# Two groups of score matmuls put side by side, with two of their tiles in another part of PSUM

## The chip, the cores and the metric

The kernel runs on one core of one Trainium2 chip. The metric is the device time of one execution in microseconds (us). Before the change it is 2308.98 us, the median of three runs (2308.58 to 2309.19).

## The reference

Two attention layers follow each other on a tensor `x` of 8 images, 32 x 32 positions (N = 1024 rows) and 256 channels, all in float32.

- Layer 0 has four heads of 256 channels each: `softmax(q k^T / 16) v` per image and head, then a product with `W_out` and the addition of `x`.
- Layer 1 has one head. Its keys `f` and queries `g` have only 32 channels, its values `h` 256: `s = g f^T`, `b = softmax(s)`, `y = gamma * (b h) + x`.

```
f, g, h = x Wf + bf, x Wg + bg, x Wh + bh
s = einsum('bik,bjk->bij', g, f)
o = einsum('bij,bjd->bid', softmax(s, axis=-1), h)
y = gamma * o + x
```

So a matmul of layer 1's scores contracts over 32 channels, a quarter of the 128 rows of TensorE's array. The product of the probabilities with the values contracts over 1024 positions.

## The kernel before, in words

**Steps.** The work is a list of steps, each a unit and a block of 512 query rows. An image has four layer-0 units (one for each head) with two blocks each; from the second image on, a layer-1 unit of the image before stands among them, with two blocks too. Its place is given by `behind`: after the second head, and for the last image at the end of the list. Layer 1 of the last image (image 7) is run by code of its own after the loop. Thus seven layer-1 units, of images 0 to 6, go through the loop, and that of image 6 is the last unit of the list: in its second block the next step, `nxt`, is None.

**Order within a step.** In every step, pieces of several stages are put on a scale with `put(tasks, *at)`: a piece with a lower number is issued earlier (line 1073 sorts them). The engines PE (TensorE), DVE (VectorE) and ACT (ScalarE) get their instructions in exactly this order, each engine its own share of it. An engine takes them one after another; what one engine waits for from another is settled by semaphores.

**Layer 1's second block (`blk == 1`).** This step holds, in its order: the accumulation of the layer-0 output of the step before last (`L700`, on DVE, at 0.5), the first group of scores (0.5), four sums for the small output product (`L691`, on DVE, 0.6 to 0.9), the first product of block 0 (1), the second group of scores (2), the next head's queries (from 2.5), the small output product (from 3), and block 0's further products (4, 6, 8).

- A group of scores is `task` inside `Layer1.scores` (line 810 on): four matmuls (L820), each with 32 of the 128 array rows and its own PSUM tile of 512 columns, then four exponentials (L829) on ACT that read these tiles. Two groups make a block's 1024 keys.
- A product is `row_products.task` (L908): eight float32 matmuls into one PSUM tile; DVE then takes the reciprocal of the row's sum (L916) and scales and adds the tile to `x` (L918). After L918 the PSUM tile is free.
- The other matmuls, of layer 0, come from `seven` (L255), with sums on DVE (L272) and copies on ACT (L278, L284). Names: `psx_q, psy_q, psz_q` are the next head's queries, `psx_o, psy_o` the small output product, `psx_y, psy_y, psz_y` layer 0's product with the values.
- GpSimd (POOL) adds up row sums over the partitions (L626) and issues the accumulating DMA (L703) after L700.

**PSUM.** Tiles are given out by two pools of one bank a tile: `ps` with six tiles and `psm` with two. `psm` holds the small products: `psx_o` and `psy_o` (with `psz_o` in the same tile), and the projections. A pool hands out its tiles in turn; the first instruction that writes a tile waits until the last reader of the tile's former content has ended.

```
y=2, yt=1, invb=1, e=2, u=2, w=1, eh=1, uh=1, eo=1, uo=1, st=2, r=8, line=4, ps=6, psm=2,
```

On TensorE every float32 matmul is recorded as two passes, each a weight load (PEld) and a matmul (PE), so eight matmuls show as x16 and the four of a score group as x8.

Of the kernel before, what the change touches and what calls it, by code (L numbers as in the profile page):

```python
# [16 lines left out]
P = 128  # L17
# [3 lines left out]
def kernel(  # L21
# [59 lines left out]
    NB = 512  # L81
# [29 lines left out]
    def tile_of(tag, shape, name):  # L111
        return pools[tag].tile(shape, F32, tag=tag, name=name)
# [340 lines left out]
    def residual(b):  # L453


        def piece(c):
            if c == 0:
                x1T_of[b] = tile_of("xT", [P, CC, N], f"x1T_{b}")
            nc.scalar.activation(
                x1T_of[b][:, c, :], xT_of[b][:, c, :], AF.Identity, bias=boutT_sb[:, c : c + 1]  # L460
            )

        return [partial(piece, c) for c in range(CC)]
# [48 lines left out]
    class Layer0:  # L512
# [46 lines left out]
        def scores(self, blk):  # L559

            half = NT // 2
            exp = partial(nc.scalar.activation, func=AF.Exp, scale=SCALE)
            tasks = []

            def p():
                if blk not in self.p:
                    self.p[blk] = tile_of("s", [P, NT, NB], f"p_{self.name}_{blk}")
                return self.p[blk]

            for g in range(0, half, 2):  # L570
                def out(j, e, g=g):
                    return p()[:, j * half + g : j * half + g + 2, ts(e, HB)]

                def after(g=g, out=out):
                    both = p()[:, half + g : half + g + 2, :]
                    exp(both, both)  # L576
                    exp(out(0, 1), out(0, 1))

                tasks += seven(
                    f"{self.name}_{blk}_{g}", NB, 2,  # L580
                    lambda number, g=g: [
                        (i, xblocks[self.b][number][:, ts(g + i, P)],
                         self.qblocks[blk][number])
                        for i in range(2)
                    ],
                    {
                        "11": partial(out, 0, 0), "12": partial(out, 0, 1),
                        "21": partial(out, 1, 0), "22": partial(out, 1, 1),
                    },
                    WIDE, exp, after,  # L590
                )
            return tasks
# [125 lines left out]
    class Layer1:  # L718
# [87 lines left out]
                ), last,  # L806
            )

        def scores(self, blk):

            n = f"{self.name}_{blk}"
            four = P // CK
            soft = Softmax(self, blk)
            exp = partial(nc.scalar.activation, func=AF.Exp, scale=self.scale)

            def task(j0):
                pms = []
                for r in range(four):
                    pm = tile_of("ps", [P, NB], f"ps_{n}_{j0 + r}")
                    nc.tensor.matmul(  # L820
                        pm,
                        lhsT=self.f[ts(r, CK), ts(j0 + r, P)],
                        rhs=self.g[ts(r, CK), ts(blk, NB)],
                        start=True,
                        stop=True,
                    )
                    pms.append(pm)
                for r, pm in enumerate(pms):
                    (exp if blk < self.direct else nc.scalar.copy)(soft.tile()[:, j0 + r, :], pm)  # L829

            tasks = [partial(task, j0) for j0 in range(0, NT, four)]
            if blk < self.direct:
                return tasks, []
            have = [
                partial(soft.have, [(j0, j0 + 2), (j0 + 2, j0 + four)])
                for j0 in range(0, NT, four)
            ]
            return tasks, have + soft.pieces()
# [115 lines left out]
    pm = tile_of("psm", [P, NB], "pm_idle")  # L954
# [27 lines left out]
    def is_l0(s):  # L982
        return s is not None and isinstance(s[0], Layer0)

    def step(k):
        return steps[k] if 0 <= k < len(steps) else None
# [4 lines left out]
    for i, (a, blk) in enumerate(steps):  # L991
        l0 = isinstance(a, Layer0)
        one, two, nxt = step(i - 1), step(i - 2), step(i + 1)
        places = []

        def put(tasks, *at):
            assert len(tasks) == len(at)
            places.extend(zip(at, range(len(places), len(places) + len(at)), tasks))

        if l0:  # L1000
            put(a.scores(blk), 0, 2, 4, 6, 8, 10)
        else:
            tasks, _ = a.scores(blk)
            put(tasks, *((0.5, 2.4) if blk == 0 else (0.5, 2)))
        if is_l0(two):
            u, k = two
            put(u.products_of[k][2:], 1 if l0 else 0)
            if nxt is None:
                put([partial(u.invert_all, k)], 2.2)
            put([partial(u.invert, k)], 3.4 if l0 else 2.7)  # L1010
            ysums, tasks, adds[i] = u.project(k)
            put(ysums, *((1.1, 1.2, 1.3, 3.3) if l0 else (1.1, 1.2, 1.3, 2.5) if blk == 0 else
                         (0.6, 0.7, 0.8, 0.9)))
            put(tasks, *((3, 5.5, 7) if l0 else (4.5, 6, 7.2) if blk == 0 else
                         (3, 5, 7) if nxt else (1.9, 3.1, 4.1)))
            if nxt is None:
                put(adds[i], 4.2)
        if i - 1 in adds:
            put(adds[i - 1], 0.5 if l0 or blk == 1 else 2.3)
        if is_l0(one):  # L1020
            u, k = one
            sums, keys = u.sums(k)
            u.products_of[k] = u.products(k)
            put(sums, *((2.1, 3.2, 4.2, 5.6) if l0 else (0.8, 2.2, 3.5, 6.1)))
            put(keys, *((6.3, 6.6, 7.6, 8.7) if l0 else (6.3, 7.6, 8.3, 8.7)))
            put(u.products_of[k][:2], *((5, 9) if l0 else (4, 5)))
        elif one is not None:
            put(one[0].products(one[1]), *((3, 5, 7, 9) if l0 else (1, 4, 6, 8) if nxt else (1, 3, 4, 8.5)))
        if i == 0:
            put(fold[0][2:] + fold[1], -2, -1, 0.5, 1.5, 2.5, 4.5, 6.5, 8.5)  # L1030
            put(first_sums[:2], 8.4, 9.4)
        if i == 1:
            put(first_sums[2:], 1.4, 3.4)
            put(fold[2], 0.5, 2.6, 3.5, 5.5, 7.5)
            put([partial(nc.vector.tensor_scalar, bh_sb, bh_sb, gamma_sb, None, ALU.mult)], 8.5)

        if l0 and blk == 0:
            put(a.query_sums(1), 3.5, 4.3, 4.4, 5.3)
        if is_l0(nxt) and blk == NBLK - 1:
            put(nxt[0].queries(), *((2.5, 4.5, 6.5) if not l0 else  # L1040
                                    (1.5, 2.5, 4.5) if is_l0(two) else (0.5, 2.5, 5.5)))
            put(nxt[0].query_sums(0), *((6.7, 6.9, 7.3, 7.6) if not l0 else
                                        (5.4, 6.4, 7.2, 7.4) if is_l0(two) else (6.4, 7.2, 7.3, 7.4)))

        if l0 and a.h == 0 and blk == 1:
            put(residual(a.b), 5.3, 7.3)
        if l0 and a.h == 0 and blk == 1 and a.b > 0:
            put(value_sums(a.b), 1.4, 2.4, 3.4, 4.4)
        if l0 and a.h == 1 and blk == 0 and a.b + 1 < B:
            load_x(a.b + 1)  # L1050
        if is_l0(nxt) and nxt[0].h == 2 and nxt[1] == 0 and nxt[0].b + 1 < B:
            moves, turned = turn_rows(nxt[0].b + 1)
            put(moves[:4], 1, 2.5, 4, 5.5)
        if l0 and a.h == 2 and a.b + 1 < B:
            if blk == 0:
                put(moves[4:], 0.5, 1.5, 2.5, 3.5)
                put(turned, 6.4, 7.4, 8.4, 9.4)
            else:
                put(key_sums(a.b + 1), 0.5, 0.6, 6.4, 7.4)

        if l0 and a.b > 0 and a.h == behind(a.b) - 1:
            if blk == 0:
                moves, turned1 = turn_back(a.b - 1)
                put(moves[:4], 3, 4.5, 6, 7.5)
            else:
                put(moves[4:], 4, 5.5, 7, 8.5)
                tasks, moves = nxt[0].queries_apart()
                put(tasks, 1.5)
                put(moves, 1.6, 1.7, 1.8, 1.9)
        if not l0 and blk == 0:  # L1070
            put(a.values("ps"), 0.9, 1, 2.3, 3, 6.5)
            put(turned1, 2.5, 2.9, 4.2, 5.1)
        for _, _, t in sorted(places, key=lambda x: x[:2]):
            t()
# [94 lines left out]
    with tc.If(bad > 0), ExitStack() as general:  # L1169
# [7 lines left out]
        for b in range(B):  # L1177
# [3 lines left out]
            for h in range(HEADS):  # L1181
                a = General0(b, h, bout_sb)
# [4 lines left out]
            a = Layer1(b)  # L1187
# [37 lines left out]
```

## Time and profile before

| what | value |
|---|---|
| median of 3 runs | 2308.98 us |
| profiled execution, its own time | 2309.19 us |
| its span, first to last instruction | 2307.3 us |
| PE busy | 2298.1 us (100%) |
| DVE busy | 1653.9 us (72%) |
| ACT busy | 579.7 us (25%) |
| POOL busy | 319.9 us (14%) |
| L820, the scores of layer 1 on PE | x256, 36.6 us busy |
| L908, the products of layer 1 on PE | x1024, 232.1 us busy |
| mean granted TensorE clock | 0.999 |

The span is what the profiler saw between the first and the last instruction; the execution's own time has 1.9 us more around it. The timeline gives, for each engine, the start in us from the span's start, the length, the line, the tiles (written, then read) and how many instructions were merged into the row; a bracket at the end is the idle time before it and what ended it. A matmul's recorded length is longer than its turn on the array, since matmuls overlap: what counts is the distance between the starts.

### The profile page before, as it was taken

The numbers are of one execution on the slowest core, as the hardware profiler recorded it, in microseconds if no ns is written. First come the engines' busy times: TensorE is split into PE (matmuls) and PEld (weight loads), VectorE is DVE, ScalarE is ACT, GpSimd is POOL, SyncE is SP. The second block draws the span as 40 slices with busy tenths as digits, with TensorE's granted clock in tenths as the row PEclk, the third lists the DMA queues.
The fourth block names the chain that finished last, engine by engine and source line by source line (L and its number), as shares of the span: only waits on it lengthen the run. The fifth ranks groups of instructions, "written<-read, shape, count | busy, mean of one in ns | idle before, by whom it ended". The sixth has DMA issues, their size and how long they took to land.

```text
span 2307.3 us, 27302 instructions
## 1 busy us (share of the span) xinstructions
PE 2298.1 (100%) x10256; PEld 1892.6 (82%) x10256; DVE 1653.9 (72%) x2951; ACT 579.7 (25%) x1009; POOL 319.9 (14%) x206
## 2 busy tenths in 40 slices
PE   9999999999999999999999999999999999999999
PEld 7888888788878888778887888878888788888877
DVE  6787787577775777657776677766777667777763
ACT  2222222222221222212232122221222222222222
POOL 0111112011120111101121011210112101111211
PEclk9999999999999999999999999999999999999999
DMA  4211123301233013220132201322113210131222
GB/s 137 33 28 25 23 39 51 74 15 28 34 51 70 15 28 47 47 62 15 28 55 43 58 15 28 58 42 55 19 24 58 42 37 19 28 46 24 40 44 62
DMA packets 240380, 94.82 MB, mean 41 GB/s; under 512 B 204464, under 2 KB 209456, under 8 KB 240240
## 3 DMA queue, kind: packets, MB, share of 16 engines
q1 hardware_dynamic: 220784, 55.23, 12.1%
q0 software_dynamic: 19456, 37.76, 9.3%
q8 instruction: 83, 1.36, 0.4%
q14 instruction: 57, 0.47, 0.1%
HBM read 29.76 MB, written 8.65 MB: 17 GB/s over the span
## 4 chain that ended last, share of the span: by engine, by line
PE 99%; DMA 1%; SPq 0%; DVE 0%; issue 0%; ACT 0%
PE psy_y L255 14%; PE psy L255 14%; PE pa_l L908 10%; PE psx L255 10%; PE psx_y L255 10%; PE psz_y L255 10%; PE psz L255 10%; PE psy_o L255 6%; PE psy_q L255 4%; PE pr_v_l L494 3%; PE psx_o L255 2%; PE psx_q L255 2%; PE psz_q L255 2%; PE ps_l L820 1%; PE pm_fg L770 1%; DMA w<-in_L_conv_W_out_dram 0%
## 5 line engine op out<-in xcount | busy, mean ns | idle before, releaser
L626 POOL PARTITION_ALL_REDUCE rb<-rs x64 | 206.6, 3228 | 1436.2 <-DVE rs L624 906.1
L255 PE MATMUL psx<-q,x0T 128*128 128x256 f32 x1024 | 263.6, 380 | 0.0
L255 PE MATMUL psy<-qs,xs 128*128 128x256 f32 x1024 | 262.9, 379 | 0.0
L255 PE MATMUL psz<-q,xs 128*128 128x256 f32 x1024 | 262.8, 379 | 0.0
L576 ACT ACTIVATE p<-p 128x1024 f32<-128x1024 f32 x128 | 135.3, 1057 | 494.6 <-DVE p L272 494.6
L255 PE MATMUL psy_y<-p,xt 128*128 128x256 f32 x1024 | 241.9, 379 | 0.0
L255 PE MATMUL psx_y<-p,x 128*128 128x256 f32 x1024 | 241.9, 379 | 0.0
L908 PE MATMUL pa_l<-v_l,s_l 128*128 128x257 f32 x1024 | 232.1, 381 | 0.0
L255 PEld LDWEIGHTS psx<-q,x0T 128*128 128x128 f32 x1024 | 193.9, 190 | 45.2 <-issue 20.7
L255 PEld LDWEIGHTS psx_y<-p,x 128*128 128x128 f32 x1024 | 194.7, 190 | 34.0 <-issue 8.6
L908 PEld LDWEIGHTS pa_l<-v_l,s_l 128*128 128x128 f32 x1024 | 193.9, 190 | 34.2 <-issue 6.8
L255 PEld LDWEIGHTS psy<-qs,xs 128*128 128x128 f32 x1024 | 194.6, 190 | 26.7 <-DVE q L272 0.4
L255 PEld LDWEIGHTS psy_y<-p,xt 128*128 128x128 f32 x1024 | 194.7, 190 | 26.3
L255 PEld LDWEIGHTS psz<-q,xs 128*128 128x128 f32 x1024 | 194.7, 190 | 26.3
L284 ACT ACTIVATE p<-psx 128x512 f32<-128x512 f32 x128 | 76.4, 597 | 363.8 <-PE psx L255 363.6
L272 DVE TENSOR_TENSOR u<-psy,e 128x512 f32<-128x512 f32 x128 | 88.1, 688 | 86.9 <-ACT e L278 75.5
L703 POOL DMA_DIRECT2D x1T<-o x64 | 78.1, 1220 | 427.2 <-DVE o L700 304.5
L255 PE MATMUL psy<-qs,x0T 128*128 128x256 f32 x512 | 132.3, 381 | 0.3 <-DVE v L272 0.3
L272 DVE TENSOR_TENSOR v<-psy,e 128x512 f32<-128x512 f32 x128 | 88.3, 690 | 53.0 <-PE psy L255 51.6
L255 PE MATMUL psy_y<-ss,xt 128*128 128x256 f32 x512 | 121.4, 380 | 0.1
L255 PE MATMUL psz_y<-ss,x 128*128 128x256 f32 x512 | 121.0, 379 | 0.0
L255 PE MATMUL psz_y<-ss,xt 128*128 128x256 f32 x512 | 121.0, 379 | 0.0
(139 smaller groups left out, 3404.6 us busy)
## 6 DMA issues: line engine op xcount, KB each, us to landing
x1T<-o POOLq DMA_DIRECT2D x64, 512.0 KB, 5.0
invb<-inv SPq DMA_DIRECT2D x63, 256.0 KB
x<-x1T SPq DMA_DIRECT2D x256, 32.0 KB
out_dram<-x SPq DMA_DIRECT2D x15, 512.0 KB
x<-in_x_dram SPq DMA_DIRECT2D x14, 512.0 KB
x0T<-x SPq DMA_DIRECT2D x224, 32.0 KB
fg<-v_l POOLq DMA_DIRECT2D x56, 64.0 KB, 2.1
w<-in_L_conv_W_qkv_dram SPq DMA_DIRECT2D x4, 512.0 KB
```

The costliest lines, as they stand in the source:

```text
L255: nc.tensor.matmul(banks[k][:, ts(i, w)], lhsT=lhsT, rhs=rhs, start=first and n == 0, stop=True, skip_group_check=True,)
L272: nc.vector.tensor_tensor(dst, shaped(banks[k]), shaped(other), ALU.add)
L284: copy(outs["11"](), shaped(banks["x"]))
L494: nc.tensor.matmul(pm[:, ts(j, C)], lhsT=src()[:, c, ts(2 * t2 + j, P)], rhs=w()[:, c, :], start=(c == 0), stop=(c == CC - 1),)
L576: exp(both, both)
L626: nc.gpsimd.partition_all_reduce(t, r.rearrange("p e i -> p (e i)"), P, bass_isa.ReduceOp.add)
L703: nc.gpsimd.dma_start(x1T_of[self.b][:, :, ts(blk, NB)], o, accum_op=ALU.add)
L770: nc.tensor.matmul(pm[ts(k, half)], lhsT=w[:, c, :], rhs=x1T_of[b][:, c, ts(k, NB)], start=(c == 0), stop=(c == CC - 1),)
L820: nc.tensor.matmul(pm, lhsT=self.f[ts(r, CK), ts(j0 + r, P)], rhs=self.g[ts(r, CK), ts(blk, NB)], start=True, stop=True,)
L908: nc.tensor.matmul(pm[:, : C + 1], lhsT=p[:, j, ts(ti, P)], rhs=v[:, j, : C + 1], start=(j == 0), stop=(j == NT - 1),)
```

## The change

Two things change for the second block of a layer-1 unit, where a next step exists:

- both groups of scores are put behind the first product, one right after the other (at 2 and 2.05 in place of 0.5 and 2);
- the first two tiles of the block's scores come from the `psm` pool in place of `ps`.

The condition holds for the units of images 0 to 5. In image 6's unit `nxt` is None, and the closing code for image 7 calls `scores` without the new argument; both stay as they were. What is computed does not change, nor the number of instructions that do it. Three lines more stand in the file, so L820 becomes L822, L829 becomes L831, L908 becomes L910, L916 and L918 become L918 and L920.

```diff
-        def scores(self, blk):
+        def scores(self, blk, small=0):
...
                 for r in range(four):
-                    pm = tile_of("ps", [P, NB], f"ps_{n}_{j0 + r}")
+                    tag = "psm" if j0 + r < small else "ps"
+                    pm = tile_of(tag, [P, NB], f"ps_{n}_{j0 + r}")
                     nc.tensor.matmul(
...
         else:
-            tasks, _ = a.scores(blk)
-            put(tasks, *((0.5, 2.4) if blk == 0 else (0.5, 2)))
+            pair = blk == 1 and nxt is not None
+            tasks, _ = a.scores(blk, 2 if pair else 0)
+            put(tasks, *((0.5, 2.4) if blk == 0 else (2, 2.05) if pair else (0.5, 2)))
```

## The prediction

> **What bounds the kernel now.** I read the page's head first, then the waits, then the timeline of each engine around one of the changed places (times below are us from the start of the span).
>
> ```profile
> span 2307.3 us, 27302 instructions
> PE 2298.1 (100%) x10256; PEld 1892.6 (82%) x10256; DVE 1653.9 (72%) x2951; ACT 579.7 (25%) x1009; POOL 319.9 (14%) x206
> ```
>
> TensorE is busy for 2298.1 of 2307.3 us, and in the list of waits no wait of PE's matmuls passes 1.1 us in its total. So there is no slack on PE: whatever PE gains or loses at one place is gained or lost at the end. The work is the same in every image: layer 1's second block begins at 400.97, 684.91, 968.84, 1252.95, 1536.89 and 1820.82, 283.9 us apart each time. The second of these, on PE:
>
> ```profile
> 684.38 0.59 PE L255 MATMUL psz_y<-ss,x 128*128 128x256 f32 x2
> 684.91 1.14 PE L820 MATMUL ps_l<-fg 32*128 32x512 f32 x8
> 685.98 3.73 PE L908 MATMUL pa_l<-v_l,s_l 128*128 128x257 f32 x16
> 689.64 1.14 PE L820 MATMUL ps_l<-fg 32*128 32x512 f32 x8
> 690.71 1.13 PE L255 MATMUL psx_q<-x0T,wqk 128*128 128x512 f32 x2
> ```
>
> See the starts: first group of scores (four float32 matmuls, two passes each), product, second group, psx_q. In VectorE's timeline of the same stretch see when it reaches the product's reader, the last line:
>
> ```profile
> 685.96 2.90 DVE L700 TENSOR_TENSOR o<-o,invb 128x1024 f32<-128x1024 f32 x1
> 688.77 0.41 DVE L691 TENSOR_TENSOR yt<-y 128x256 f32<-128x256 f32 x1
> 689.22 0.42 DVE L691 TENSOR_TENSOR y<-y 128x256 f32<-128x256 f32 x1
> 689.68 0.42 DVE L691 TENSOR_TENSOR yt<-y 128x256 f32<-128x256 f32 x1
> 690.13 0.42 DVE L691 TENSOR_TENSOR yt<-y,yt 128x256 f32<-128x256 f32 x1
> 690.48 0.16 DVE L916 RECIPROCAL inverse<-pa_l 128x1 f32<-128x1 f32 x1
> 690.67 0.48 DVE L918 SCALAR_TENSOR_TENSOR x<-pa_l,inverse,x 128x256 f32<-128x256 f32 x1
> ```
>
> GpSimd's, ScalarE's and the weight loads' timelines have the rest: the reduction that L700 runs beside, the exponentials, and the load of psy_q, the matmul that today takes over the product's bank:
>
> ```profile
> 685.54 3.23 POOL L626 PARTITION_ALL_REDUCE rb<-rs  x1 [15.99 <-issue]
> 686.11 2.06 ACT L829 ACTIVATE s_l<-ps_l 128x512 f32<-128x512 f32 x4 [7.25 <-PE ps_l L820]
> 690.80 2.06 ACT L829 ACTIVATE s_l<-ps_l 128x512 f32<-128x512 f32 x4 [2.62 <-PE ps_l L820]
> 691.27 0.19 PEld L255 LDWEIGHTS psy_q<-xs,wt 128*128 128x128 f32 x1 [0.27 <-issue]
> ```
>
> [...] In mid-stream a 512-column matmul of two passes takes 0.86 us (698.15 to 699.01) and a product 3.46 us (694.69 to 698.15); here the product takes 3.66 us (685.98 to 689.64), 0.11 more for a weight load that nothing hides [...]. [...] L700 takes 1.22 us as a rule (median 1216 ns) and 2.90 us here, ending just after the reduction does (685.54 + 3.23 = 688.77).
>
> **What is removed.** A group in four row tiles costs, beyond its two passes: 0.09 drain + 1.07 (684.91 to 685.98) + 0.11 load of the next full-array matmul - 0.86 = 0.41 us. With both groups side by side one way in and one way out fall away. What a seam between two groups of one mode costs, no row shows: at least 0 (the second pass's loads inside a group are hidden already), at most the 0.11 of an open load. I take 0; it is hidden in the wait below in any case. If nothing waited, the gain is 0.41 us a place (0.30 at the other end), and places there are six: images 0 to 5. Image 6's second block is the last step (nxt is None) and image 7 goes through the closing code; both keep the old form. 6 x 0.41 = 2.5 us.
>
> **What is added: a wait for the product's bank.** PSUM's ps pool has six tiles and hands them round in turn. After the change pa_l takes one, then come ps_l 2 and 3 of the first group and ps_l 4 to 7 of the second, since only 0 and 1 go to psm: with pa_l as number one, ps_l 7 is number seven and gets pa_l's bank. (The built program agrees: exactly this matmul has a wait on VectorE and TensorE that was psy_q's before; there psy_q was seventh.) That bank is free when L918 has read it. VectorE's order of work is the same instruction by instruction, and nothing ahead of L918 in it waits for a PE instruction later than psz_y, so L918 ends when it does now, at 690.67 + 0.48 = 691.16 to the nearest reading. It is late because VectorE first finishes L700, held up by GpSimd, and four L691, not because of the product.
>
> PE in the new order:
> - psz_y's stream ends at 684.82 (eight of 0.216 from 683.09). The product follows with no change of mode and ends its stream at 684.82 + 3.46 = 688.28.
> - Drain 0.09, first group's load at 688.37, streaming 688.48 to 689.34.
> - The second group's tiles 4 to 6 can start; ps_l 7 cannot. Its load begins at 691.16 + 0.11 = 691.27 (0.11 is what lay between L918's end and psy_q's load in the trace of before).
> - From the first load of a group to the next full-array load is 1.07: psx_q's load at 692.34.
>
> Before, that load was at 690.71. Each place loses 692.34 - 690.71 = 1.63 us: a wait of 2.04 (689.23, when the load would have begun without a wait, to 691.27) less the 0.41. The bounds: the release by semaphore could take 0.05 or 0.2 instead of 0.11, and the seam or a split of the passes 0.1: 1.5 to 1.8.
>
> Behind the held matmul stands everything on PE: psx_q, psy_q, the o products, the next pa_l. Their readers have room. ScalarE's four exponentials of the first group run at 689.57 to 691.64 (1.20 after the load, as now); those of the second begin near 692.5, end near 694.5, and the copy of psx_q behind them moves from 692.72 to about 694.5. VectorE's u_q needs the copy, at about 695.1 instead of 693.38; the matmul that needs u_q, the second psy_q, comes at 699.01 + 1.63 = 700.64. All banks taken over later are freed by these exponentials in time. The moved step issues no DMA; the queues of SP and POOL keep their order, and POOL's accumulating DMA (L703) follows L700, which stays. No later stall is there today that the delay could fall into, so nothing is given back.
>
> Sum: 6 x 1.63 = 9.8 us. The profiled execution took 2309.19 us, its span 2307.3 (1.9 around it); it becomes 2319.0, span 2317.1. The median of the runs is 2308.98, 0.21 lower, so 2318.8 us, 0.42% slower.
>
> **Rivals.**
> - *Exponentials, not the product's reader, set the stall.* If L918 came early (were L700 not held by the reduction, it would end 1.68 sooner, at 689.48), psx_q would still take ps_l 2's bank, freed by the first group's third exponential, which ends at 688.37 + 2.78 = 691.15 (2.78 from a group's first load to that end, as now). PE is due for psx_q's load at 690.30 and gets it at 691.26: 0.55 lost, 6 x 0.55 = 3.3, time 2312.3. This is within 0.2%, not slower by that measure. It decides when L918 ends before about 690.08; against it, the 2.90 us is in all six places (2.895 to 2.899), and that reduction's start depends on VectorE alone.
> - *Neither wait binds.* Both releases fall within their cover: L918 before 689.1 and the third exponential before 690.2. Then 2308.98 - 2.5 = 2306.5. For it speaks only that 0.41 us a place is really there; against it, L918 is 2 us and the exponential 1 us beyond those points.
> - *The idle array slows.* [...] The new idle is at most 2.04 us[...]; the mean granted clock here is 0.999, through gaps of up to 0.83 us early on, so the trace does not test it. [...]
>
> **How the numbers follow.** The held second group 0.86, with its own range 6 x 1.5 to 6 x 1.8: 2318.0 to 2319.8, widened by the 0.3 of run to run on each side. Exponentials alone 0.05; no wait 0.03; slowed clock 0.06. The range for 8 in 10 is the first case with a margin for a size I misread by a third of a microsecond a place: 2316 to 2322. What this measurement can tell from no change is about 0.2%, 4.6 us. Slower: first and last case, 0.92; same: the two middle ones, 0.07 (+3.3 and -2.5 both lie within 4.6); faster 0.01.
>
> **What would show it.** Right: at six places the product begins some 0.09 after psz_y's last matmul's turn, at 684.82 in place of 685.98 in the second; L918 still at about 690.7; ScalarE's first four exponentials at 689.6; a PE gap of some two microseconds inside L822's second group, put down to VectorE x or its reciprocal; psx_q at 692.3; L700 still 2.90; images 0 to 5 each longer by 1.6 us, from 283.9 to 285.6 apart; image 6 and the end as before. Wrong: L822 as one unbroken block, or psx_q waiting for ACT s_l; a granted clock under 1.0 would speak for the last rival. The forecast fails if the held matmul does not hold the group behind it, or if VectorE reaches L918 at another time than now.

## The result and the profile after

The changed kernel takes 2321.71 us, the median of four runs (2317.99 to 2325.29), against 2308.84 for the kernel before on the same chip: a ratio of 1.0056, 95% interval 1.0044 to 1.0068. It is slower by half a per cent; 2318.8 (2316 to 2322) was predicted. The profiled execution is the lowest of the four, 2317.99 us, with a span of 2316.1.

The head of its page:

```profile
span 2316.1 us, 27296 instructions
PE 2301.8 (99%) x10256; PEld 1894.3 (82%) x10256; DVE 1655.1 (71%) x2951; ACT 579.4 (25%) x1009; POOL 319.9 (14%) x206
```

In its list of waits PE's matmuls have a first entry that they did not have before, with the six places in its count (total us, times, longest us):

```profile
PE ps_l L822 <- DVE x L920: 5.7, 6, 0.9
```

The second place again, from the timelines of PE, weight loads, VectorE, ScalarE and GpSimd (start and length in us):

```profile
684.40 1.89 PE L255 MATMUL psz_y<-ss,x 128*128 128x256 f32 x8
686.12 3.63 PE L910 MATMUL pa_l<-v_l,s_l 128*128 128x257 f32 x16
689.68 1.99 PE L822 MATMUL ps_l<-fg 32*128 32x512 f32 x14
692.62 1.09 PE L822 MATMUL ps_l<-fg 32*128 32x512 f32 x2 [0.94 <-DVE x L920]
693.64 1.12 PE L255 MATMUL psx_q<-x0T,wqk 128*128 128x512 f32 x2
...
692.59 0.29 PEld L822 LDWEIGHTS ps_l<-fg 32*128 32x128 f32 x2 [1.74 <-PE ps_l L822]
...
687.27 2.90 DVE L700 TENSOR_TENSOR o<-o,invb 128x1024 f32<-128x1024 f32 x1
...
691.45 0.43 DVE L691 TENSOR_TENSOR yt<-y,yt 128x256 f32<-128x256 f32 x1
691.79 0.16 DVE L918 RECIPROCAL inverse<-pa_l 128x1 f32<-128x1 f32 x1
691.99 0.48 DVE L920 SCALAR_TENSOR_TENSOR x<-pa_l,inverse,x 128x256 f32<-128x256 f32 x1
...
690.84 4.03 ACT L831 ACTIVATE s_l<-ps_l 128x512 f32<-128x512 f32 x8 [10.66 <-PE ps_l L822]
694.80 0.59 ACT L278 COPY e_q<-psx_q 128x512 f32<-128x512 f32 x1
...
686.85 3.23 POOL L626 PARTITION_ALL_REDUCE rb<-rs  x1 [15.99 <-issue]
```

See that the two groups make one row of 14 matmuls: both passes of the first group and of tiles 4 to 6 of the second. Only the two passes of ps_l 7 stand apart, at 692.62, and they wait for VectorE's L920, which ends at 691.99 + 0.48 = 692.47; the load of ps_l 7 starts 0.12 later, at 692.59. L700 still takes 2.90 us beside the reduction. The row gives 0.94 for the gap because a matmul's recorded length overlaps its successor; by the starts, tile 7's matmul comes 2.94 us after the pair's first, and would come 0.98 after it with nothing to wait for (as in e4 below).

The distance from psz_y's last matmul to psx_q's first, by their starts, holds the whole place. It was 6.115 us and is 7.736: 1.62 more, within 0.01 at all six places, 9.73 in the sum. The span grows by 8.8 only: the first place happens to begin 0.31 earlier in this execution, 0.18 comes back between the places (nearly all of it in one image, which was 0.17 longer than the others in the trace of before), and the time from the last matmul to the end is 0.46 shorter.

So the predicted mechanism is there at its predicted size, in the one execution that the profile shows. What it does not explain is the 7.3 us between the lowest and the highest run, where the kernel before had 0.6. The experiments had to settle both.

### The profile page after: what moved, and what is told of

The parts are those of the page before. It is cut to its first block, busy times and chain, and to the rows that moved or that the text cites. A ratio compares the mean times of both kernels' runs of the same rounds, so it can differ in the third digit from the quotient of the medians.

```text
span 2316.1 us, 27296 instructions
## 1 busy us (share of the span) xinstructions
PE 2301.8 (99%) x10256; PEld 1894.3 (82%) x10256; DVE 1655.1 (71%) x2951; ACT 579.4 (25%) x1009; POOL 319.9 (14%) x206
## 4 chain that ended last, share of the span: by engine, by line
PE 95%; DVE 3%; DMA 1%; issue 0%; SPq 0%; ACT 0%; DVEq 0%
PE psy L255 14%; PE psy_y L255 14%; PE psx L255 10%; PE psz L255 10%; PE psx_y L255 9%; PE psz_y L255 9%; PE pa_l L910 9%; PE psy_o L255 6%; PE psy_q L255 4%; PE psx_q L255 2%; PE psz_q L255 2%; PE psx_o L255 2%; PE pr_v_l L494 2%; PE ps_l L822 1%; DVE o L700 1%; PE pm_fg L770 1%
## 5 line engine op out<-in xcount | busy, mean ns | idle before, releaser
L910 PE MATMUL pa_l<-v_l,s_l 128*128 128x257 f32 x1024 | 231.4, 380 | 0.0
L910 PEld LDWEIGHTS pa_l<-v_l,s_l 128*128 128x128 f32 x1024 | 194.2, 190 | 30.0 <-issue 2.3
```

What stands on the lines that cost most here:

```text
L910: nc.tensor.matmul(pm[:, : C + 1], lhsT=p[:, j, ts(ti, P)], rhs=v[:, j, : C + 1], start=(j == 0), stop=(j == NT - 1),)
```

## The experiments

The theory after the result: ps_l 7 waits for the bank of pa_l, whose reader is behind L700 and the four L691 on VectorE. Against it stood the rivals on record, two that end near no change and one of a slower clock, and the question what makes some runs longer. In the diffs below the lines ahead are those of the changed kernel, unless said otherwise.

### The same kernel again

e1 is the changed kernel itself, without an edit, so that there is a profile of another of its executions.

> The changed kernel unchanged, for its spread: its four runs lay at 2318.0, 2321.7, 2321.7 and 2325.3 us, steps of 3.65 us, with mean clocks of 1.0, 0.998, 0.998 and 0.997. If the bank wait alone makes the time, all runs lie at 2318.5 or so within 0.3 us. If the array's clock is halved now and then because of the wait, the runs lie on a ladder 2318.0 + n x 3.65 us, and a run's mean clock falls by some 0.001 to 0.0015 with each step.

Measured: 2325.21 us (2320.55 to 2325.51), before 2308.88, ratio 1.0063 (1.0049 to 1.0076). The profiled execution is of the long ones, 2325.45. The view by stretches of time shows why (in order: from and to, length, busy time and instructions of PE, PEld, DVE, ACT and POOL, then the granted clock, the share of the DMA engines and GB/s):

```profile
693.00:696.20 3.20, 2.25 (x13) 0.70 (x7) 1.71 (x5) 3.02 (x7) 1.02 (x1) 1.00 0.64 102
696.25:699.66 3.41, 3.41 (x5) 1.36 (x5) 0.01 (x1) 1.54 (x3) 0.00 (x0) 0.50 0.83 107
699.66:703.00 3.34, 3.34 (x15) 2.53 (x15) 1.19 (x3) 0.37 (x1) 0.00 (x0) 1.00 0.33 49
```

And PE's timeline in the same stretch:

```profile
694.96 1.09 PE L822 MATMUL ps_l<-fg 32*128 32x512 f32 x2 [0.94 <-DVE x L920]
695.98 1.85 PE L255 MATMUL psx_q<-x0T,wqk 128*128 128x512 f32 x2
697.63 1.92 PE L255 MATMUL psy_q<-xs,wt 128*128 128x512 f32 x2
```

The place itself is as in the first profile (the held matmul 2.94 us after the pair's first, psx_q at 3.96), but psx_q and psy_q behind it run at half speed: psx_q to psy_q is 1.65 us instead of 0.96. The trace's clock records have one stretch of 3.412 us at half clock behind four of the six places (from 409.53, 696.25, 1269.69 and 1556.41), and none behind the other two. Each costs half of its length, 1.71 us: four make 6.8, and the place's start in image 0 is 0.65 later, which is together the 7.5 us between the two spans (2323.6 and 2316.1). In the profiled execution of the first measurement there is no such stretch. The other runs fit the same ladder: 2318 plus 0, 1, 2 or 4 times 1.7 comes within a microsecond of all nine; the step of some 3.65 between the first four runs is two windows at once. For the runs without a trace, which have only a time and a mean clock, it is an inference.

So the third rival does happen, in part. The stretches lie on a grid of 3.413 us that does not follow the kernel: their starts are 286.72, 573.44 and 286.72 us apart, which is 84, 168 and 84 times 3.4133, while the places of that trace are 285.55 or 287.25 us apart. The clock records of the two other profiles have the same step: full clock from 3.98 to 2314.81 us in the first profile of the changed kernel, 677 times 3.4133, and from 4.36 to 2304.95 in that of the kernel before, 674 times, each time followed by half clock, after PE's last matmul. Where a grid window, one step of it, begins at a place without a half-speed stretch is an estimate, counted on in steps of 3.4133 from the ends that such records show. With the pair's first load as zero, the array has little to do in a low stretch: from 1.82 (end of tiles 4 to 6) to 2.94 it is idle, and then to 3.96 it works on one tile of 32 rows. In the same measure (+0.81 is 0.81 us after the pair's first load) a half-speed window followed in e1 where a grid window began at +0.81, +0.91, +1.34 and +1.44, and not at +0.27 or +0.38; in the first profile none at +0.38, +0.46, +1.54 and +1.63 (at the other two places of that profile windows began at +2.63 and +2.71). Where the grid falls thus has a part in it: all four windows with half speed behind them hold the low stretch whole, and those from +0.27, +0.38 and +0.46 cut off its end. But it does not settle it: the windows from +1.54 and +1.63 hold the stretch whole too, and nothing followed. The stretch is 2.1 us, of which only 1.1 is idle by the distances of the matmuls, much less than a window.

### The pair without the small pool

e2 leaves the order and gives all eight tiles to `ps`, as before the change.

```diff
-            tasks, _ = a.scores(blk, 2 if pair else 0)
+            tasks, _ = a.scores(blk, 0)
```

> Both groups behind the product, but all eight tiles from the six of the ps pool. If the bank of the product decides, one score tile (now ps_l 5, the seventh after pa_l) waits for the same VectorE instruction, the first group's exponentials that ps_l 6 and 7 need end before it, and psx_q follows at the same distance: 1.62 us lost a place, the lowest run at 2318.0 us as with the change. If the two psm tiles were what matters (for good or ill), the time differs from that by more than 1 us.

Measured: 2322.97 us (2320.54 to 2325.35), ratio 1.0062 (1.0046 to 1.0077). PE's timeline at the second place:

```profile
690.25 1.98 PE L822 MATMUL ps_l<-fg 32*128 32x512 f32 x10
693.19 1.13 PE L822 MATMUL ps_l<-fg 32*128 32x512 f32 x6 [0.96 <-DVE x L920]
```

Now ten matmuls go ahead and six are held: ps_l 5 is the seventh tile from pa_l, so the wait falls on tile 5 and holds 5 to 7. It ends at the same 2.94 us after the first load; the place is 7.78 us long instead of 7.74. The trace has two half-speed windows (from 1551.68 and 1838.40), after grid windows that began at +1.22 and +0.65; one at +1.28 had none behind it. The lowest run, 2320.54, is not at the 2318.0 that was expected; its mean clock of 0.999 is that of e1's run of 2320.55, so one half-speed window would account for it, which without a trace is again an inference. The two tiles from `psm` thus change which tile is held, and hardly the time.

### The small pool without the pair

e3 has the opposite half: groups where they were before, two tiles from `psm`.

```diff
-            put(tasks, *((0.5, 2.4) if blk == 0 else (2, 2.05) if pair else (0.5, 2)))
+            put(tasks, *((0.5, 2.4) if blk == 0 else (0.5, 2)))
```

> Two of the second block's tiles from psm, the groups at their old places. If the bank of the product decides: nothing, 2308.8 us within 0.5, since pa_l's bank is taken over by psy_q as before. If the tiles in psm hurt the small products or the first group waits for their readers: slower by a wait that shows in front of L822's first group or of psx_o.

Measured: 2308.98 us (2308.3 to 2309.56), ratio 1.0000 (0.9992 to 1.0009). This half costs nothing where the groups stand apart; all of the loss comes with the pair.

### VectorE reads the product first

e4 keeps the change and moves VectorE's work behind the reader: L700 from 0.5 to 1.2 and the four L691 from 0.6 and on to 1.3 and on. Nothing moves on PE. If L700 holds the release, this takes the wait away, and what remains is the wait for the exponentials. L700 and the sums move together here; what each of them adds to the delay is read from the timelines, not from runs of their own.

```diff
-                         (0.6, 0.7, 0.8, 0.9)))
+                         (1.3, 1.4, 1.5, 1.6) if nxt is not None else (0.6, 0.7, 0.8, 0.9)))
...
-            put(adds[i - 1], 0.5 if l0 or blk == 1 else 2.3)
+            put(adds[i - 1], 1.2 if not l0 and blk == 1 and nxt is not None else 0.5 if l0 or blk == 1 else 2.3)
```

> The change, and VectorE's order turned round in these six steps: the product's reader (reciprocal and L920) comes before L700 and the four L691. If the product's bank, read late, is the cause, the wait goes from the seventh score tile; what is left is the third exponential's hold on psx_q, 0.55 us a place against before: 2308.8 + 3.3 = 2312.1 us, with PE's gap of about 0.96 us in front of psx_q put down to ACT s_l. If side by side costs by itself (mode, seams, the psm tiles), the time stays near 2318 us. If nothing but the reader mattered: 2308.8 - 2.5 = 2306.3. If waits of about 2 us are what halves the clock, the runs here have no steps of 3.65 us.

Measured: 2311.53 us (2311.3 to 2312.12 in 21 runs), ratio 1.0012 (1.0005 to 1.0018). Timelines of PE and VectorE at the second place:

```profile
689.11 2.03 PE L822 MATMUL ps_l<-fg 32*128 32x512 f32 x16
691.89 1.12 PE L255 MATMUL psx_q<-x0T,wqk 128*128 128x512 f32 x2 [0.75 <-ACT s_l L831]
...
689.42 0.48 DVE L920 SCALAR_TENSOR_TENSOR x<-pa_l,inverse,x 128x256 f32<-128x256 f32 x1
689.82 1.22 DVE L700 TENSOR_TENSOR o<-o,invb 128x1024 f32<-128x1024 f32 x1
```

All sixteen matmuls are one block, L920 ends at 689.90, and now psx_q waits, for an exponential: exactly the first rival's picture. The place is 6.562 us long, 0.45 more than before, where 0.55 was expected. ScalarE's third exponential ends at 691.84, 2.73 after the pair's first load, and psx_q's load follows 0.05 later; 2.78 and 0.11 had been reckoned. No window is at half speed, and the runs lie within 0.8 us of each other. L700, which begins after the reduction's end (GpSimd runs it from 686.28 for 3.23, to 689.51), takes 1.22 instead of 2.90.

### The release of psx_q too: another tile in the small pool

e6 is e4 with the two `psm` tiles moved from score tiles 0 and 1 to 2 and 3. Then psx_q, eighth in `ps` from pa_l, takes the bank of ps_l 0, whose exponential is the first to end, instead of ps_l 2's.

```diff
-                    tag = "psm" if j0 + r < small else "ps"
+                    tag = "psm" if small and j0 + r in (2, 3) else "ps"
```

> As the run with the reader first, but the third and fourth score tile are the ones from psm, so psx_q takes over the bank of the first exponential (ends 1.76 us after the first load) in place of the third's (2.73). If the exponential's hold on psx_q is what was left of the loss, it goes; psz_q still waits for the fifth exponential, some 0.11: 0.26 us a place gained against before, 2308.85 - 1.5 = 2307.3. If the exponentials did not matter, the time stays at 2311.5.

Measured: 2307.32 us (2306.88 to 2308.46), before 2309.3, ratio 0.9993 (0.9984 to 1.0001). PE's timeline at the second place:

```profile
688.44 2.03 PE L822 MATMUL ps_l<-fg 32*128 32x512 f32 x16
690.41 1.12 PE L255 MATMUL psx_q<-x0T,wqk 128*128 128x512 f32 x2
691.37 1.02 PE L255 MATMUL psy_q<-xs,wt 128*128 128x512 f32 x2
692.26 1.12 PE L255 MATMUL psz_q<-xs,wt 128*128 128x512 f32 x2
693.22 0.59 PE L255 MATMUL psx_o<-y,wvo 128*128 128x256 f32 x2
```

The wait of psx_q is gone: it follows 1.97 us after the pair's first load, and the place is 5.738 us long, 0.377 shorter than before. Up to there this is the gain of 0.41 that the prediction had reckoned for the side-by-side groups, seen without its waits. A small wait is left behind it, the one that was expected: psz_q takes the bank of the fifth exponential, which ends at 692.21, and its load comes 0.05 later. From psy_q to psx_o PE takes 1.85 us by the starts, where the kernel before takes 1.72. From psz_y's last matmul to the next product it is 9.85 us, against 10.09 before: 0.24 gained a place, 1.4 in all, near the 0.26 that was reckoned. e10 is e6 again, on another chip:

> The kernel of e6 unchanged, in more rounds on another occasion: 2309.0 - 6 x 0.377 = 2306.7 by the place's own distance in its trace, 2307.3 by its median; the ratio to the kernel before 0.9990 to 0.9993, below 1 with its interval. If the gain was chance of the chip, the ratio is 1.000.

Measured: 2307.58 us (2307.0 to 2307.89), before 2309.39, ratio 0.9992 (0.9983 to 1.0). Both intervals reach 1.0, so neither alone excludes no change. That both come out alike, that the places are shorter in both traces (by the same 0.24), and that all 13 runs of e10 lie below all 33 of the kernel before on that chip (2308.53 to 2310.2) speaks for a gain. The gains of 2.0 and 1.8 us are 0.4 to 0.5 above what the places account for, which was not followed up.

### The small output product first

e5 is e4 with another cure for the wait for the exponentials: the small output product (psx_o, in `psm`) goes ahead of the next head's queries, and L700 goes to 1.7.

```diff
-                         (3, 5, 7) if nxt else (1.9, 3.1, 4.1)))
+                         (2.3, 5, 7) if nxt else (1.9, 3.1, 4.1)))
```

> The change, with the product's reader first on VectorE (then the four L691, then L700) and on PE the small output product ahead of the queries behind the second group. psx_o then takes over the bank of the first exponential and psy_o that of the second, which end 1.76 and 2.25 us after the pair's first load, before PE comes for them (1.99 and 2.42). If waits for banks are the whole cost, none is left, and what side by side saves shows at last: 0.37 to 0.41 us a place, 2308.85 - 2.3 = 2306.6 us, all runs within 0.6 us. If side by side saves nothing, 2308.9.

Measured: 2313.34 us (2312.27 to 2316.8), ratio 1.0019 (1.0012 to 1.0027): a miss. At the place it does what was expected (5.738 us from psz_y to psx_o, no wait). The loss is some 28 us later; timelines of PE and VectorE there:

```profile
718.52 1.13 PE L255 MATMUL psy<-qs,x0T 128*128 128x256 f32 x4 [0.90 <-DVE v L272]
...
716.64 1.22 DVE L700 TENSOR_TENSOR o<-o,invb 128x1024 f32<-128x1024 f32 x1 [4.27 <-DMA invb<-inv]
717.78 0.68 DVE L272 TENSOR_TENSOR v<-psy,e 128x512 f32<-128x512 f32 x1
```

The next L700 waits for the row of reciprocals (invb) that a DMA brings, v stands behind it on VectorE, and PE's psy waits for v. The DMA is late in SP's queue. The new order puts 13 of the copies of x0T ahead of the copy of inv, where the kernel before has 11. From psz_y's last matmul on, inv's copy is issued at 18.1 us instead of 17.1, and invb's, which stands behind it, at 26.9 instead of 25.7.

e9 puts that back: the task that takes the reciprocal of the sums and issues these two copies (L642 to L649) goes from 2.7 to 2.45, ahead of another batch of x0T copies, so that 10 are in front. (The reciprocal itself is not late: in e5 VectorE has it at 694.9, 7.6 us before SP issues its copy.)

```diff
-            put([partial(u.invert, k)], 3.4 if l0 else 2.7)
+            put([partial(u.invert, k)], 3.4 if l0 else 2.7 if blk == 0 or nxt is None else 2.45)
```

> The kernel of e5 with layer 1's call of the reciprocal of the sums at 2.45 instead of 2.7, so that 10 copies of x0T instead of 13 stand ahead of the copy of inv in SP's queue (11 in the kernel before). If the lateness of inv and invb in SP's queue is what cost e5 its gain, the place keeps its 0.377 us and the waits some 28 us later (0.9 to 2.6 us a place) go: 2309.2 - 6 x 0.38 = 2306.9. If VectorE's own order (the scaling L700 after the small product's sums) makes v late, the waits stay and the time is again near 2313.

Measured: 2306.62 us (2306.04 to 2307.37 in 20 runs), before 2309.39, ratio 0.9988 (0.9981 to 0.9995). SP's timeline of e5, inv and invb:

```profile
702.55 0.55 SPq L647 DMA_DIRECT2D inv<-inverse  x1
...
711.29 0.34 SPq L649 DMA_DIRECT2D invb<-inv  x1
```

The same of e9:

```profile
700.97 0.55 SPq L647 DMA_DIRECT2D inv<-inverse  x1
...
709.65 0.34 SPq L649 DMA_DIRECT2D invb<-inv  x1
```

Weight loads' waits for v, of e5 and then of e9 (total us, times, longest us):

```profile
PEld psy L255 <- DVE v L272: 11.0, 13, 2.6
```

```profile
PEld psy L255 <- DVE v L272: 2.9, 7, 0.6
```

The waits go from 11.0 us to 2.9, less than the kernel before has (3.3), with VectorE's order of L700 and v unchanged. So SP's queue was the cause, and e9 is the fastest kernel of this study, 2.8 us under the kernel before. The six places account for 2.3 of them: here nothing waits up to the next product, which comes 9.71 us after psz_y's last matmul, 0.38 earlier than before. Where the other 0.5 comes from was not followed up here either.

### The idle array kept busy

e7 asks whether it is the idle array that halves the clock. It is the changed kernel with the matmuls of tiles 4 to 6 repeated, with the same operands and the same result, in the time in which tile 7 waits.

```diff
+                    if small and j0 > 0 and r == 2:
+                        for k in range(3):
+                            nc.tensor.matmul(
+                                pms[k],
+                                lhsT=self.f[ts(k, CK), ts(j0 + k, P)],
...
```

> The change, with the matmuls of score tiles 4 to 6 done twice while ps_l 7 waits (extra work with the same result, 0.86 us of it inside the wait). The wait for the bank is as long as before. If the halved clock comes from the array being idle through most of a 3.41 us window, it no longer comes: all runs at 2318.2 us within 0.6, mean clock 1.0. If a held wait or three quarters of the rows being idle is what counts, the ladder of 1.7 us steps stays, up to 2325 us. If the extra matmuls lengthen the wait, each 0.1 us shows as 0.6.

Measured: 2319.57 us (2319.23 to 2320.12), ratio 1.0046 (1.0032 to 1.0059). PE's timeline at the second place, the repeated matmuls on L832 and the held tile behind them:

```profile
690.17 1.99 PE L822 MATMUL ps_l<-fg 32*128 32x512 f32 x14
691.99 1.03 PE L832 MATMUL ps_l<-fg 32*128 32x512 f32 x6
693.10 1.09 PE L822 MATMUL ps_l<-fg 32*128 32x512 f32 x2
```

The wait is the same: tile 7's matmul comes 2.93 us after the pair's first, and the place is 7.73 us long. But the ladder is gone: five runs lie within 0.9 us, each with a mean clock of 1.0, and the trace has no half-speed window at the places, though grid windows began at +1.23 and +1.47, near those that e1 had halved behind them (+1.34, +1.44). Filling 0.86 us of the 1.1 us of idle time is enough here. The median is 1.4 us above the 2318.2 that was expected. In the trace that is not at the places: the first of them begins 0.50 later than in the first profile, and two of the stretches between them are 0.35 and 0.51 longer.

### A later reader

e8 makes the wait longer: two reductions over 512 columns, whose result nobody uses, stand ahead of the reader on VectorE.

```diff
+        if not l0 and blk == 1 and nxt is not None:
+            late = tile_of("r", [P, 1], f"late{i}")
+            put([partial(nc.vector.tensor_reduce, late, wh_sb.rearrange("p c d -> p (c d)"), op=ALU.add, axis=AX.X)] * 2, 0.95, 0.96)
```

> The change, with two idle reductions of 512 columns (0.69 us each, an estimate from additions of that width) put in front of the product's reader on VectorE in the six steps. If PE waits for this reader, each 0.1 us goes straight into the time: 1.38 us a place, 8.3 in all, so 2318.2 + 8.3 = 2326.5 with no halved window. If a wait of some 3.8 us halves the clock in more places than one of 2.4, some 4 of 6 windows at 1.7: 2333 us or more. If the reader is not what PE waits for, the time stays at 2318 to 2325.

Measured: 2344.1 us (2328.77 to 2344.93), ratio 1.0129 (1.0101 to 1.0157). PE's timeline at the second place:

```profile
693.37 1.99 PE L822 MATMUL ps_l<-fg 32*128 32x512 f32 x14
697.61 1.82 PE L822 MATMUL ps_l<-fg 32*128 32x512 f32 x2 [2.25 <-DVE x L920]
699.36 2.08 PE L255 MATMUL psx_q<-x0T,wqk 128*128 128x512 f32 x2
```

The held matmul moves from 2.94 to 4.25 us after the pair's first, by 1.31, which is what the two reductions take on VectorE by their starts. So the reader's time carries over to PE one for one. The rest is the clock: one half-speed window at the first place, whose grid window began at +2.90 and holds only a part of the idle time, and two in succession, 6.827 us, at each of the other five, where a window began between +0.78 and +1.07 and holds all of it. 2316.1 of the changed kernel's span, 6 x 1.31 = 7.9 and 11 x 1.71 = 18.8 make 2342.8; the span is 2343.1. The run of 2328.77 has no trace; its time fits one window or two, and its mean clock of 0.999 is that of the runs with one.

## Why the prediction was right, and where it was not

**The wait for the product's bank: right, in every term.** With the pair's first load as zero (688.37 predicted, 689.68 in the profile, the difference being the first place's loss less 0.31 of an earlier start):

| step | predicted | measured |
|---|---|---|
| psz_y's last start to the pair's first load, no change of mode ahead of the product | 3.77 | 3.77 |
| L920 ends | 2.79 | 2.79 |
| held load of ps_l 7 | 2.90 | 2.91 |
| psx_q's load | 3.97 | 3.96 |
| loss of a place | 1.63 | 1.62 |

That it is L920 that binds is shown from both sides: with the reader earlier the wait goes (e4), with the reader 1.31 later it is 1.31 longer (e8). That it is tile 7, by the count of the six `ps` tiles, is shown by e2, where without the two `psm` tiles it is tile 5. The seam between the groups was taken as 0: after the change the second group's first matmul comes 0.96 after the first group's, which is 0.53 to the second pass and 0.43 for its stream, and in e6, with no wait up to psx_q, the place gains 0.377 of the 0.41. The 0.09 that the prediction's sums call drain is a distance, from the end of psz_y's stream by its reckoning (684.82) to the first group's start (684.91); what TensorE does in it no run shows. That the held matmul holds all that stands behind it on PE, which the prediction took as given, is in the timelines: psx_q comes 1.05 after the held load in the profile (3.96 and 2.91), and none of the matmuls behind passes tile 7, in e8 not in a wait of 2.25 us either.

**The exponentials as the next in line: right, with a size off by 0.10.** With the product's reader out of the way, psx_q waits for the third exponential (e4). The term was 0.55 a place and measured 0.45: the exponential ends 0.05 earlier than reckoned and its release takes 0.05 and not 0.11, which was VectorE's. With 0.45 that rival's sum is 2308.98 + 6 x 0.45 = 2311.7; e4 took 2311.53.

**What ScalarE does with the second group: wrong, without effect.** Its exponentials were put at 692.5, as if all four tiles were held. Tiles 4 to 6 were not, as the same working says two paragraphs above, so the eight exponentials run without a break (4.03 us in one row) and psx_q's copy comes about 1 us earlier than reckoned, in the place's own time. Nothing waited for it.

**The idle array slows: the step that failed.** The chance of 0.06 was wrong. It was given with a bound for the new idle of 2.04 us, but the trace of before has no gap on PE behind its first matmul over 0.83 us and could not say what 2 us do; that they would be harmless was the author's estimate. The runs show it: a half-speed window is 3.41 us long and costs 1.71 (e1), and one could follow a grid window that held some 1.1 us without a matmul and 1 us with one quarter of the rows in use. And because the grid does not follow the kernel (the places are 83.66 or 84.16 steps of 3.4133 apart) the choice was not between all places and none: 0 to 4 of the six were hit in an execution. So the likeliest time was not 2318.8 but a ladder from there upwards, with a median of 2321.7 in the first measurement and 2325.2 in e1. The predicted range held the first and not the second; its upper end came from misreadings of the wait, not from the clock. That the first median lay inside it, 0.3 us below its end, was luck: the bank wait as predicted makes the lowest run, 2317.99, with no half-speed window in its trace. The other 3.7 us of that median come, by the mean clock of 0.998 in the two runs that make it, from half-speed windows, the rival with the chance of 0.06.

What stays open is what exactly brings the half clock. The window positions above do not give it away: +1.44 was followed by half speed and +1.54 and +0.46 were not, +1.22 was in e2 and +1.28 was not. That an idle stretch alone need not do it is seen in e4: there PE is idle from 1.88 to 2.79, with full-array matmuls behind, grid windows from +0.41, +0.60 and +1.48 hold that whole, and no half speed followed. An experiment that sweeps the length of an idle stretch against the grid wasn't tried.

**The gain that the change could have had: 0.38 a place,** 2.3 us, near the second rival's 2.5 (2306.5). It needs two things that the change does not bring: the reader ahead of L700 on VectorE, and behind the pair only matmuls whose banks are freed early. e6 and e10 have the first and most of the second (psz_q still waits, so 0.24 a place) and end at 0.9993 and 0.9992 of the time before; e9 has both and ends at 0.9988.

**L700 beside the reduction: the prediction read more than the trace shows.** In the trace of before, the seven L700 that run beside a reduction of GpSimd's take 2.895 to 2.899 us, the other 57 1.214 to 1.227; with the reader first (e4) L700 begins behind the reduction and takes 1.22. So L700 is slower beside it, while the reduction takes 3.23 us with L700 beside it or without. How L700 is held up is not shown. It ends 0.085 us after the reduction's recorded end (688.851 and 688.766), where some 1.2 would be due if it had been shut out up to then. How long the one really holds up the other stays open, since the ends recorded for GpSimd are rough. What L700 saves in e4 did not show in the time on its own: VectorE has room (71% busy).

## What to carry to other kernels

Before a PE stage is moved, count which tile of the pool its writes will take over, and read from the reader's engine what stands ahead of that tile's last reader: here a slow scaling that no one on PE waited for became the wait of all six places, and putting two pieces of VectorE's list behind the reader took it away. A wait of 2 us on PE is not only its own length: here it could bring 3.4 us of half clock behind it, in some executions and not in others, so look at the spread of the runs and the clock records, not at one profile. When tasks change places, count the DMAs between two links of a chain in each queue: in e5 two more copies ahead of one small one cost more than the whole gain. And follow the chain to the next big piece of work, not only to the first matmul: in e6 a second, smaller wait stands two matmuls further on.

## What was not expected of the hardware

- TensorE's clock was halved for one window of 3.41 us behind six of the nine grid windows that held a low stretch with 1.1 us of idle time whole (all four in e1, two of three in e2, none of two in the first profile), and for two windows in succession at five places with 2.4 us idle (6.83 us in e8). Where three repeated matmuls in the 32-row tiles filled 0.86 of the 1.1 us of idle time, it was not (mean clock 1.0 in all five runs of e7).
- A matmul in row tiles that waits for its bank does not hold the passes of the tiles issued ahead of it: tiles 4 to 6 end both passes while tile 7 waits (14 matmuls in one row from 689.68 to 691.67, the held one from 692.62).
- A bank freed by ScalarE was taken by PE's load 0.05 us after the exponential's recorded end (e4), one freed by VectorE 0.12 after L920's.
